# Two layers of image-prompt cross-attention: even entries with their image tokens first, three value groups instead of four where two token tiles can share one, and five score products instead of six

## The chip, the core and the metric

The kernel runs on one core of a Trainium2 chip. The core has five instruction streams that the profile names: PE (TensorE, matrix products; its weight loads are listed apart as PEld), DVE (VectorE), ACT (ScalarE), POOL (GpSimd) and SP (SyncE, which here only issues DMAs). Data lies in SBUF (128 partitions), products land in PSUM banks, and DMAs move data between SBUF and DRAM. The metric is the time of one execution on the device in microseconds (us).

## What is computed

The reference runs two attention layers over a batch of B = 16 entries with S = 256 queries, 20 heads of 16 dimensions, and a context of 256 tokens per entry (512 features). The time goes to these lines; the first layer is

```python
text = encoder_hidden_states[:, :TEXT_LEN]     # TEXT_LEN = 77
ip = encoder_hidden_states[:, TEXT_LEN:]       # 179 image tokens
q = hidden_states @ Wq
k_text, v_text = text @ Wk, text @ Wv
logits = einsum('bhqd,bhkd->bhqk', q_h, k_h) * scale
text_out = softmax(logits) @ v_h
ip_k, ip_v = ip @ Wk_ip, ip @ Wv_ip
scores = einsum('bhqd,bhkd->bhqk', q_h, ip_k_h) * scale
text_probs = softmax(q @ k_text.T * scale)     # over all 320 columns, no heads
q_sem = text_probs @ text
sem = (q_sem @ ip.T) * scale
ip_probs = softmax(scores + SEM_SCALE * sem) * spatial_mask
out = (text_out + ip_probs @ ip_v_h) @ Wout + bout + hidden_states
```

The second layer takes this output, has 252 text and 4 image tokens, and uses a similar semantic term on normalized vectors. So in layer one an entry's 256 context tokens are 77 that go through the text weights (Wk, Wv) and 179 that go through the image weights (Wk_ip, Wv_ip).

## The kernel before, in words

**Numbers.** A product of two 32-bit arrays is made from rounded halves: each array is split into a high part `hi` and a rest `lo`, and `prod` sums hi·hi, hi·lo and lo·hi over the blocks of the contraction; with 4 blocks of 128 features that is 12 products for one result. ACT writes the high part (`nc.scalar.copy`), DVE or POOL subtracts it to get the rest (`halves`). The last 64 of the 320 projected columns are stored as 64 high and 64 low weight columns side by side, so that a third block of columns (`m == 2`) gives both halves of its result in the two halves of the partitions; `evacuate` adds them.

**Stages.** `begin` loads the first weights and context and computes the first two entries by hand order. Layer one then runs in 80 slots (16 entries times 5 groups of 4 heads, `slot0`), layer two in 80 more (`slot1`). The name slot is a clock for a list of tasks: each task is a generator with a table of slot numbers, and `fill` runs every step that has come due. PE's order is fixed by this program order (`PINNED`), while the order of ACT, DVE, POOL and SP is chosen at build time by a scheduler that simulates the program.

**A slot of layer one.** For group `k` it does, in this order on PE: the transposed score products T of the first 128 tokens (`turned0`, tokens on partitions, queries along the row), a few task steps, the value products P·V of the group before (`attend0`, 24 products in sets of 4 side by side), the score products S of group `k + 2` (`score0`, queries on partitions, only to take the row maxima), T of the other 128 tokens, again task steps, and the small transposition of the maxima (`maxima0`). For S, DVE takes two maxima per head, one over text and one over image tokens. Four small DMAs on ACT's queue write the maxima as two more rows of the query stack (`qs`), where indicator rows of the key stack (`ks`) pick the right one. For T, ACT takes the exponential into a tile P and POOL multiplies it with `rs`, the exponential of the semantic term, so that P·V can follow. `settle0` transposes the result on DVE, divides by the sums, and POOL adds the text half and the image half into `hsn`; for the fifth group POOL copies that block once more (`hsn[:, 2, :, 1]`), and `gather` transposes `hsn` on DVE for the output projection (`finish`, PE lines 610 and 613, DVE lines 284 and 285).

**Token tiles.** An entry's 256 tokens stand text first, image behind. The first tile of 128 tokens holds 77 text and 51 image tokens, the second 128 image tokens. The value rows of the mixed tile are made twice, once with the text weights and once with the image weights, and a mask per partition keeps the right rows (`tmask`): three groups of 12 products per entry (`values0_`), six per pair. Columns 16, 33, ... of a value tile hold the mask itself and give the sums.

**Per pair of entries** (`c`, two entries of 512 tokens): `context` loads the context features in four chunks of 128x512 and splits them into `cta` and `ctb` (ACT high, POOL rest), `keys0` makes the key projections (three column blocks, text with 156 columns, image with 360) into `kst`, copies the text keys into `kb` on POOL, and writes `kst` to DRAM (`keys_out`), from where `stacks0` loads it in head order into `ks`. `tokens0` makes the 77x179 matrix M of text by image features (12 products of 192 columns), whose transposes give `rs`. `semantic0` makes the text scores over all 320 columns: per half of the queries six products (three column blocks, high and low of q) of 156 columns.

## Time and profile before

| what | value |
|---|---|
| median of 3 runs | 1497.43 us (1495.08 to 1497.73) |
| the profiled execution's own time | 1499.52 us |
| its span | 1497.7 us |
| PE instructions | 12740 products |
| layer one's slots after the start-up | from about 100 us to about 690 us |
| layer two's slots | about 700 us to 1450 us |

Engine rows give busy time in us, its share of the span and the count of instructions. In rows of groups the columns are: line and engine, operation, output <- inputs, shape, count, busy us in total, mean ns of one, and behind the bar the engine's idle time just before these instructions with what ended it. The mean ns of a product is its whole passage, and products overlap; the pace is read from the chain of waits, whose rows are start in us, length in us, engine, output, line and count of a run. In tables of stretches each engine has its busy us and its count of instructions, then the clock granted to PE, the busy share of the DMA engines and GB/s.

### The profile page before, as it was taken

The numbers are of one execution on the slowest core, as the hardware profiler recorded it, in microseconds if no ns is written. First come the engines' busy times: TensorE is split into PE (matmuls) and PEld (weight loads), VectorE is DVE, ScalarE is ACT, GpSimd is POOL, SyncE is SP. The second block draws the span as 40 slices with busy tenths as digits, with TensorE's granted clock in tenths as the row PEclk, the third lists the DMA queues.
The fourth block names the chain that finished last, engine by engine and source line by source line (L and its number), as shares of the span: only waits on it lengthen the run. The fifth ranks groups of instructions, "written<-read, shape, count | busy, mean of one in ns | idle before, by whom it ended". The sixth has DMA issues, their size and how long they took to land.

```text
span 1497.7 us, 36123 instructions
## 1 busy us (share of the span) xinstructions
PE 1427.8 (95%) x12740; PEld 1155.6 (77%) x12740; DVE 1170.2 (78%) x2593; ACT 884.8 (59%) x1975; POOL 1215.2 (81%) x1304
## 2 busy tenths in 40 slices
PE   8789999999999899789999999999999999999997
PEld 8678888888888778577777777777777777777765
DVE  5467777777777787878887788778877887788785
ACT  5346565656565555556666666666666666666562
POOL 4259797979797977887698879887988798879786
PEclk9799999999999999999999999999999999999999
DMA  7767787778787776775434434443444344433411
GB/s 237 201 185 217 201 228 200 217 206 224 199 231 193 219 200 173 186 216 150 145 102 132 127 108 128 127 127 108 127 128 127 109 126 129 127 108 103 122 26 39
DMA packets 230986, 234.32 MB, mean 156 GB/s; under 512 B 39127, under 2 KB 200678, under 8 KB 230790
## 3 DMA queue, kind: packets, MB, share of 16 engines
q1 hardware_dynamic: 228598, 230.71, 55.4%
q8 instruction: 102, 1.67, 0.5%
q10 hardware_dynamic: 2208, 1.30, 0.4%
q14 instruction: 78, 0.64, 0.1%
HBM read 118.04 MB, written 77.04 MB: 130 GB/s over the span
## 4 chain that ended last, share of the span: by engine, by line
PE 73%; DVE 8%; DMA 6%; POOL 6%; issue 3%; ACT 3%; SPq 1%; ACTq 0%; DVEq 0%; POOLq 0%
PE X L942 15%; PE X L240 14%; PE P L804 6%; PE X L610 5%; PE P L954 5%; PE S L745 5%; PE P L964 4%; PE T L769 4%; PE T L894 3%; PE S L900 3%; PE X L613 2%; PE X L250 2%; PE X L579 2%; POOL P L775 2%; DVE mn L747 1%
## 5 line engine op out<-in xcount | busy, mean ns | idle before, releaser
L775 POOL TENSOR_TENSOR P<-P,rs 128x512 f32<-128x512 f32 x320 | 414.4, 1318 | 90.2 <-ACT P L772 89.3
L933 POOL TENSOR_TENSOR wt<-P,ctb 128x512 f32<-128x512 f32 x320 | 410.6, 1308 | 72.8 <-ACT ctb L932 72.8
L942 PE MATMUL X<-ctb,gm 128*128 128x512 f32 x1120 | 305.4, 402 | 5.8 <-DVE wt L943 5.7
L772 ACT ACTIVATE P<-T 128x512 f32<-128x512 f32 x320 | 175.4, 594 | 159.5 <-PE T L769 101.9
L943 DVE TENSOR_TENSOR wt<-X,wt 128x512 f32<-128x512 f32 x320 | 216.1, 680 | 42.7 <-PE X L942 36.4
L942 PEld LDWEIGHTS X<-ctb,gm 128*128 128x128 f32 x1120 | 195.3, 188 | 39.0 <-DVE wt L943 8.7
L914 ACT ACTIVATE P<-T 128x512 f32<-128x512 f32 x320 | 173.0, 593 | 76.2 <-PE T L894 73.3
L932 ACT ACTIVATE ctb<-P 128x512 fp32r<-128x512 f32 x320 | 186.7, 627 | 36.8 <-PE X L942 33.1
L902 DVE TENSOR_REDUCE mn<-S 128x4 fp32r<-128x1008 f32 x160 | 191.3, 1196 | 0.0
L747 DVE TENSOR_REDUCE mn<-S 128x4 fp32r<-128x716 f32 x160 | 142.2, 889 | 0.0
L804 PE MATMUL P<-P,vr 128*32 128x256 f32 x1920 | 127.4, 396 | 5.3 <-DVE tmp L821 2.0
L745 PE MATMUL S<-ks,qs 125*128 125x256 f32 x640 | 117.7, 307 | 4.9 <-DMA ks<-M 2.8
L745 PEld LDWEIGHTS S<-ks,qs 125*128 125x128 f32 x640 | 89.0, 195 | 40.1 <-issue 20.9
L1031 POOL TENSOR_TENSOR r<-u,rs 128x40 f32<-128x40 f32 (+2 forms) x17 | 108.7, 6394 | 3.9 <-DVE u L1028 3.9
L769 PE MATMUL T<-qs,ks 127*128 127x256 f32 x640 | 108.2, 292 | 0.4 <-DMA qs<-mt 0.4
L746 DVE TENSOR_REDUCE mn<-S 128x4 fp32r<-128x308 f32 x160 | 74.4, 465 | 31.2 <-PE S L745 30.8
L815 DVE STREAM_TRANSPOSE nt<-P 128x512 f32<-128x512 f32 x80 | 56.9, 711 | 51.8 <-PE P L804 51.3
L769 PEld LDWEIGHTS T<-qs,ks 127*128 127x128 f32 x640 | 92.1, 198 | 2.0 <-DMA qs<-mt 1.0
L804 PEld LDWEIGHTS P<-P,vr 128*32 128x32 f32 x1920 | 57.2, 112 | 47.0 <-issue 8.1
L954 PE MATMUL P<-P,v1t 128*32 128x256 f32 x1280 | 85.7, 385 | 0.0
L964 PE MATMUL P<-wt,zone 128*32 128x256 f32 x1280 | 85.1, 381 | 0.3 <-DVE wt L943 0.3
L610 PE MATMUL X<-ho,wF 128*128 128x256 f32 x512 | 74.3, 287 | 6.5 <-ACT mt L755 4.0
(297 smaller groups left out, 2974.5 us busy)
## 6 DMA issues: line engine op xcount, KB each, us to landing
qd<-q SPq DMA_DIRECT2D x96, 256.0 KB
qs<-tph SPq DMA_DIRECT2D x64, 320.0 KB
rawc<-in_cT_dram SPq DMA_DIRECT2D x60, 256.0 KB
qs<-qd SPq DMA_DIRECT2D x80, 192.0 KB
ks<-kd SPq DMA_DIRECT2D x80, 192.0 KB
ks<-kd SPq DMA_DIRECT2D x160, 96.0 KB
qs<-qd SPq DMA_DIRECT2D x160, 96.0 KB
kd<-kst SPq DMA_DIRECT2D x57, 256.0 KB
```

The source lines that it names most:

```text
L240: last = mm(out, lhs(a, k), rhs(b, k), start=i == 0, stop=i == len(terms) - 1)
L745: mm(sp[:, h], Q[: XROW + T0, h, t * 128 : (t + 1) * 128], K[: XROW + T0, h], start=True, stop=True)
L769: mm(st[p][:, j], K[:KS0, 2 * p + j, t * 128 : (t + 1) * 128], Q[:KS0, 2 * p + j], start=True, stop=True)
L772: exp = anchor(nc.scalar.activation(pt, st[p], AF.Exp, scale=SCALE))
L775: anchor(nc.gpsimd.tensor_mul(pt, pt, rs[:, t : t + 1].to_broadcast([128, 2, S])))
L804: mm(pv[32 * s : 32 * s + 32, o : o + S], v[:, vt, h : h + 32], P[k, s // 2][:, t, s % 2], start=vt < 2, stop=vt != 1,)
L902: anchor(nc.vector.tensor_reduce(maxes[k + 2][:, t], sp[:, :, :T1], axis=AX.X, op=ALU.max))
L914: anchor(nc.scalar.activation(P[k, u][:, t], st[u], AF.Exp, scale=SCALE))
L932: nc.scalar.activation(R[k, u][:, t], P[k, u][:, t], AF.Copy, scale=0.5)
L933: anchor(nc.gpsimd.tensor_sub(W[k, u][:, t], P[k, u][:, t], f(R[k, u][:, t])))
L942: mm(yp, gm[:, gb], R[k, u][:, kt], start=i == 0, stop=i == len(blocks[n]) - 1)
L943: nc.vector.tensor_mul(W[k, u][:, n], yp, W[k, u][:, n])
```

## The change

Even entries of layer one are laid out with their 179 image tokens first and the 77 text tokens behind; odd entries stay text first. The even entry's second tile then holds 51 image tokens (rows 0 to 50) and 77 text tokens (rows 51 to 127), the odd entry's first tile 77 text tokens and 51 image tokens (rows 77 to 127). One group of 12 products whose 128 tokens are 51 image tokens of the even entry, 26 columns of zeros and 51 image tokens of the odd entry serves both mixed tiles (`values_mixed`); its result is evacuated twice, with the even and with the odd mask. To make these 128 tokens lie side by side, the context tiles get a layout of their own (51 zeros, then per half: text, text, image, 26 zeros, image, one zero), so the split into halves is done in two pieces per chunk, and image keys are evacuated entry by entry. `ks` gets 77 more columns: an even entry's key stack starts 77 columns later, so that the image columns of both layouts lie on the same place and the constant rows stay. Six other edits come along: the semantic scores use five products, since the last block of q now holds its high and low parts in the two halves of the partitions (and `kb` its text keys twice, by 8 small POOL copies instead of 3); M's product has 180 columns instead of 192; M's zeros are written once at the start instead of once per entry; the mask columns of the value tiles are written per entry (`mark`) instead of once; and the fifth group's block is written doubled by one DVE instruction, in layer one as the sum itself, in layer two as the product, instead of by a POOL copy.

```diff
@@ values
-        for t, (w,), lo, sc in ((0, wv0, 0, tmask[:, 0:1]), (1, wvi0, 0, tmask[:, 1:2]), (2, wvi0, 128, 1.0)):
-            prod(vp, lambda s, k: ct(s, k)[:, i, lo : lo + 128], lambda s, k: w(s, k), 4)
...
+    def value_rows(ct, at, w, *to):
+        vp = bank()[:, :320]
+        prod(vp, lambda s, k: side(ct[k], s, at, 128), lambda s, k: w(s, k), 4)
+        for V, t, sc in to:
             nc.scalar.activation(
                 vcols(V, V0W)[:, t, :, 0:16], vp.rearrange("p (h d) -> p h d", d=D), AF.Copy, scale=sc
             )
+    def values0_(b):
+        ct, i = ct0[b // 2], b % 2
+        V = mark(b)
+        value_rows(ct, T0 if i else -MIX, wv0[0], (V, 0, masks(b)[0]))
+        yield
+        value_rows(ct, CI + (CG + MIX if i else 0), wvi0[0], (V, 2, 1.0))
+        yield
         return V
+    def values_mixed(c):
+        to = [(vr[(b + 2) % 3], 1, masks(b)[1]) for b in (2 * c, 2 * c + 1)]
+        value_rows(ct0[c], CI + 128, wvi0[0], *to)
+        yield
@@ halves of a projected block
+    def evacuate(hi, lo, out, m, pieces=None, beside=False):
+        cut = [lambda t, b=b: t[:, b] for b in pieces] if pieces else [lambda t: t]
+        if m == 2:
+            hi, lo = hi[:64], hi[64:] if beside else lo[:64]
+            both = buf("both", list(hi.shape), bufs=2)
+        for of in cut:
+            nc.scalar.copy(of(hi), of(out[:64] if m == 2 else out))
...
+        for of in cut:
+            nc.vector.tensor_sub(of(out if m == 2 else lo), of(out), f(of(hi)))
@@ split of the context
+                if isinstance(hi, list):
+                    for piece in zip(hi, lo, by_side(src)):
+                        halves(*piece, eng, "pieces")
@@ keys
-                    nc.gpsimd.tensor_copy(kt[:n, m, :, :, :T0], f(kst[:n, :, :, :T0]))
+                    for h in range(2):
+                        for p in range(0, 128, n):
+                            nc.gpsimd.tensor_copy(kt[p : p + n, m, h, :, :T0], f(texts(kst)[:n, h]))
@@ M
-        nc.gpsimd.memset(f(M[:, :, :T0]), 0.0)
-        lo = 64
-        prod(gp[:T0, : S - lo], lambda s, k: ct(s, k)[:, i, :T0], lambda s, k: ct(s, k)[:, i, lo:S], 4)
+        prod(gp[:T0, : S - T0 + 1], lambda s, k: texts_of(ct[k], s)[:, i], lambda s, k: images_of(ct[k], s, 1)[:, i], 4)
@@ semantic scores
-            for k in range(3):
-                qt = lambda h: qh[:, h, k, t * 128 : (t + 1) * 128]
-                for h in range(2):
-                    mm(sf[:, : 2 * NT].rearrange("p (s n) -> p s n", s=2), qt(h), kt[:, k], start=k + h == 0, stop=k + h == 3)
+            for k, h in ((0, 0), (0, 1), (1, 0), (1, 1), (2, 0)):
+                qt = qh[:, h, k, t * 128 : (t + 1) * 128]
+                mm(sf[:, : 2 * NT].rearrange("p (s n) -> p s n", s=2), qt, kt[:, k], start=k + h == 0, stop=k == 2)
@@ stacks and scores
-        Q, K = QK[k] = qs[k % SIZES["NR"]], ks[k % SIZES["NR"]]
+        Q, K = QK[k] = qs[k % SIZES["NR"]], (ks if b % 2 else turned_ks)[k % SIZES["NR"]]
...
+        text, image = (slice(0, T0), slice(T0, S)) if k // NG % 2 else (slice(S - T0, S), slice(0, S - T0))
@@ P·V
-        for vt in range(3):
-            values0(k, pv, v, vt)
+        get("vm", b // 2)
+        for step in ((0, 0, 0, 1, 1), (1, 0, S, 1, 0), (2, 1, S, 0, 1)) if b % 2 else ((2, 0, S, 1, 0), (1, 1, S, 0, 1), (0, 1, 0, 1, 1)):
+            values0(k, pv, v, *step)
@@ settle0
-        nc.gpsimd.tensor_add(hn[:, g // 2, :, g % 2], tmp[:, 0], tmp[:, 1])
         if g == NG - 1:
-            nc.gpsimd.tensor_copy(hn[:, 2, :, 1], hn[:, 2, :, 0])
+            nc.vector.tensor_add(hn[:, 2], *[tmp[:, i].unsqueeze(2).to_broadcast([128, 8, 2, 16]) for i in range(2)])
             later(0.45, lambda: gather(0, b))
+        else:
+            nc.gpsimd.tensor_add(hn[:, g // 2, :, g % 2], tmp[:, 0], tmp[:, 1])
@@ settle1
         if g == NG - 1:
-            nc.gpsimd.tensor_copy(hn[:, 2, :, 1], hn[:, 2, :, 0])
+            wide = lambda t: t.unsqueeze(2).to_broadcast([128, 8, 2, 16])
+            nc.vector.tensor_mul(hn[:, 2], wide(na[:, :, 0:16]), rz.unsqueeze(2).unsqueeze(3).to_broadcast([128, 8, 2, 16]))
@@ the table of slots
-        task(("v0", 2 * c), shifted(n, -7, -5.4, -5), lambda b=2 * c: values0_(b), *k)
-        task(("v0", 2 * c + 1), shifted(n, -4, -3.8, -3.4), lambda b=2 * c + 1: values0_(b), *k)
+        task(("v0", 2 * c), shifted(n, -7, -5.4), lambda b=2 * c: values0_(b), *k)
+        task(("vm", c), shifted(n, -4.2), lambda c=c: values_mixed(c), *k)
+        task(("v0", 2 * c + 1), shifted(n, -3.8, -3.4), lambda b=2 * c + 1: values0_(b), ("vm", c))
```

The order of the instructions moves at three places that the prediction speaks of. Rows give the line, the operation, output <- inputs and the shape; `x3` is a run of three alike.

First PE, where the even entry of a pair got its two image value groups between a T and the transposition of the maxima (`wD` holds the image value weights, `cta` and `ctb` the context, `X` is a PSUM bank, `S` and `T` are the score products). Before:

```order
L769 MATMUL T_67<-qs2_97,ks2_101 128x256 x2
L240 MATMUL X_2214<-wD_93,cta_0_81 128x320 x3
L240 MATMUL X_2214<-wD_93,cta_1_82 128x320 x3
L240 MATMUL X_2214<-wD_94,ctb_0_83 128x320 x3
L240 MATMUL X_2214<-wD_94,ctb_1_84 128x320 x3
L240 MATMUL X_2230<-wD_93,cta_0_81 128x320 x3
L240 MATMUL X_2230<-wD_93,cta_1_82 128x320 x3
L240 MATMUL X_2230<-wD_94,ctb_0_83 128x320 x3
L240 MATMUL X_2230<-wD_94,ctb_1_84 128x320 x3
L753 MATMUL X_2248<-ident_r_79,mn_0_566 8x128 x2
L745 MATMUL S_66<-ks1_100,qs1_96 128x256 x4
```

and now:

```order
L861 MATMUL T_67<-qs2_97,ks2_101 128x256 x2
L251 MATMUL X_2265<-wD_93,cta_0_81 128x320 x3
L251 MATMUL X_2265<-wD_93,cta_1_82 128x320 x3
L251 MATMUL X_2265<-wD_94,ctb_0_83 128x320 x3
L251 MATMUL X_2265<-wD_94,ctb_1_84 128x320 x3
L845 MATMUL X_2285<-ident_r_79,mn_0_613 8x128 x2
L836 MATMUL S_66<-ks1_100,qs1_96 128x256 x4
```

One of two groups of 12 is gone there; the rest of PE's order in the slot is the same.

Second DVE, after the last group of an odd entry, around the transposition `hT` of the collected result `hsn` (`mn` are the maxima of S, `nt` and `tmp` belong to `settle0`, `ho` is the split of `hT` for the output projection). Before:

```order
L747 TENSOR_REDUCE mn_0_566<-S_66 128x4
L818 RECIPROCAL P_69<-nt_0_135 128x16
L834 STREAM_TRANSPOSE hT_0_1300<-hsn_109 128x256
L819 TENSOR_TENSOR P_69<-P_69,mk_106 128x8
L821 TENSOR_TENSOR tmp_1_808<-nt_0_135,P_69 128x256
L284 TENSOR_TENSOR ho_0_161<-hT_0_1300,ho_0_161 128x512
```

and now:

```order
L913 TENSOR_TENSOR tmp_0_847<-nt_1_137,P_69 128x256
L327 SCALAR_TENSOR_TENSOR hq_0_268<-hq_0_268,tmask_80,xq_0_91 128x256
L780 TENSOR_TENSOR tph_0_303<-X_1326,tph_0_303 77x256
L915 TENSOR_TENSOR hsn_110<-tmp_0_847 128x256
L838 TENSOR_REDUCE mn_0_613<-S_66 128x4
L839 TENSOR_REDUCE mn_0_613<-S_66 128x4
L927 STREAM_TRANSPOSE hT_0_1333<-hsn_110 128x256
L326 TENSOR_TENSOR ho_0_193<-hT_0_1333,ho_0_193 128x512
```

The sum for the fifth group is now DVE's own instruction (`hsn<-tmp`), and the last `hT` and `ho` come half a slot earlier in DVE's order.

Third SP, the queue of loads for the next groups (`x1d` takes layer one's output of an entry, `ks` and `qs` are the stacks). Before:

```order
L85 DMA ks_100<-kd_70 48x4x256
L85 DMA qs_96<-qd_1418 48x1024
L85 DMA x1d<-xc_116 128x3x256
L85 DMA ks_101<-M_261 80x4x179
L85 DMA ks_101<-kd_70 48x4x256
L85 DMA xq_91<-in_xT_dram 128x3x256
L85 DMA qs_97<-tph_264 80x4x256
L85 DMA qs_97<-qd_1418 48x1024
```

and now:

```order
L89 DMA qs_96<-qd_1456 48x1024
L89 DMA ks_101<-M_173 80x4x179
L89 DMA ks_101<-kd_70 48x4x256
L89 DMA xq_91<-in_xT_dram 128x3x256
L89 DMA qs_97<-tph_304 80x4x256
L89 DMA qs_97<-qd_1456 48x1024
L89 DMA x1d<-xc_117 128x3x256
L89 DMA ks_102<-kd_70 48x4x256
```

The output of an even entry is now issued behind five loads of the next group's stacks instead of ahead of them.

188 lines of the change are left out of this document (120 added, 68 removed).

## The prediction

> **What bounds the kernel now.** I read the page's busy times first, then busy time by stage, then single slots of one pair in layer one, and last the chain of waits there.
>
> ```profile
> span 1497.7 us, 36123 instructions
> ...
> PE 1427.8 (95%) x12740; PEld 1155.6 (77%) x12740; DVE 1170.2 (78%) x2593; ACT 884.8 (59%) x1975; POOL 1215.2 (81%) x1304
> ```
>
> PE is busy 95% of the span and POOL, next, 81%. The second view says where PE is not busy:
>
> ```profile
> 0.00:100.00 100.00, 79.35 (x531) 70.82 (x531) 54.88 (x142) 47.08 (x118) 43.50 (x66) 0.91 0.77 219
> 100.00:550.00 450.00, 438.93 (x4138) 378.19 (x4136) 346.62 (x811) 262.96 (x619) 391.56 (x380) 0.99 0.76 210
> 550.00:700.00 150.00, 131.34 (x1205) 105.03 (x1204) 116.66 (x259) 82.72 (x192) 124.33 (x145) 0.94 0.68 184
> 700.00:1450.00 750.00, 741.22 (x6606) 575.53 (x6606) 623.09 (x1319) 475.98 (x1016) 620.85 (x674) 1.00 0.42 118
> ```
>
> From 100 to 550 us layer one runs evenly: PE works 438.93 of 450 us. Start-up (79.35 of 100) and the passage to layer two (131.34 of 150) have the gaps. So a product that leaves PE between 100 and 550 us shortens the kernel, if the other engines keep up in the shorter slot. The third view is ten slots of one pair; three of them, and the sum of the ten:
>
> ```profile
> 307.70:315.10 7.40, 6.58 (x65) 5.78 (x63) 7.32 (x15) 4.66 (x10) 5.84 (x6) 1.00 0.76 201
> ...
> 330.00:337.40 7.40, 7.40 (x73) 6.47 (x72) 3.90 (x10) 3.58 (x9) 5.14 (x6) 1.00 1.01 266
> ...
> 344.90:352.40 7.50, 7.45 (x73) 6.46 (x72) 6.10 (x13) 5.61 (x12) 7.46 (x9) 1.00 0.72 199
> ...
> sum 74.50, PE 72.81 PEld 63.18 DVE 57.42 ACT 43.54 POOL 64.91; mean PE 7.28 PEld 6.32 DVE 5.74 ACT 4.35 POOL 6.49
> ```
>
> A pair lasts 74.5 us. PE's share is 72.81, POOL's 64.91, DVE's 57.42. But single slots differ: DVE is full from 307.7 (7.32 of 7.40, and PE loses 0.82 there), POOL from 344.9 (7.46 of 7.50). Now the chain around the place where the order of PE loses a group (value products are `L240 x12` or `x24`, the semantic scores `L667`):
>
> ```profile
> 241.17 2.86 PE X L240 x24
> 244.16 0.53 PE S L745 x4
> ...
> 248.68 1.30 PE X L667 x12
> 250.10 0.52 PE S L745 x4
> ...
> 254.27 3.52 PE X L240 x24
> 257.91 0.53 PE S L745 x4
> ```
>
> The chain goes through PE from slot to slot, and both kinds of removed products lie on it. One slot, S to S, takes 257.91 − 250.10 = 7.81 us with the two value groups in it, and 250.10 − 244.16 = 5.94 with the semantic scores.
>
> **The change part by part.** *Value groups.* 24 products of 320 columns take 3.52 us, 147 ns each. A pair loses one group of 12: 12 × 0.147 = **1.76 us**.
>
> *Semantic scores.* 12 products of 156 columns take 1.30 us, 108 ns each. A pair loses one of six per half of the queries, in two halves and two entries: 4 × 0.108 = **0.43**. The 128-row block that replaces a 64-row one costs the same columns.
>
> *M.* 24 products per pair get 180 columns instead of 192. At 3.52/24/320 = 0.46 ns a column that is 24 × 12 × 0.46 ns = 0.13; where the pace is set by the weights, as 108 ns for 156 columns (0.69 a column) suggests, it is nothing. Between 0 and 0.13 I take 0.12, as 192 columns lie on the long side of those 156. Text keys of 154 columns instead of 156: nothing.
>
> Sum on PE: 1.76 + 0.43 + 0.12 = **2.3 us a pair**, 18.5 over eight pairs, if all of it reaches the end.
>
> *POOL.* These are the prices; T's products with `rs` (`L775`), the sum into `hsn` (`L822`), its copy (`L824`), and the small work:
>
> ```profile
> L775 POOL TENSOR_TENSOR P<-P,rs 128x512 f32<-128x512 f32 x319 | 413.1, 1318 | 81.9 <-ACT P L772 80.9
> L822 POOL TENSOR_TENSOR hsn<-tmp 128x128 f32<-128x128 f32 x80 | 41.0, 513 | 5.6 <-DVE tmp L821 5.1 <-DVE mx L674 0.5
> L168 POOL TENSOR_TENSOR cta<-rawc,cta 128x512 fp32r<-128x512 f32 x16 | 21.6, 1354 | 0.0
> L385 POOL CAST kb<-kst 128x308 fp32r<-128x308 f32 x14 | 6.2, 441 | 0.8 <-DVE rn L460 0.8
> L824 POOL COPY hsn<-hsn 128x128 f32<-128x128 f32 x16 | 4.8, 300 | 0.1
> L435 POOL MEMSET M<- 77x154 f32 x12 | 2.7, 227 | 5.0 <-PE X L697 4.8
> ```
>
> A split chunk of 512 columns becomes two pieces of 154 and 358: the columns are the same, so each of four chunks costs one more start of an instruction, at most the 0.227 of the smallest row: +0.9. Three casts of `kb` (441) become eight of half the size, each between 0.227 and 0.3 (the copy of 128 columns): +0.5 to +1.1. Four copies of mask columns (128x20): 4 × 0.227 = +0.9. Gone are two copies (0.60), two sums (1.03) and two memsets of M (0.45): −2.08. POOL gets **+0.2 to +0.8 a pair**, against 74.5 − 64.91 = 9.6 idle. Per slot POOL needs four products and a sum, 4 × 1.318 + 0.513 = 5.79. The slot that loses 1.76 shrinks to 7.81 − 1.76 = 6.05, still 0.26 above, and one of 5.94 passes already. POOL's idle time in this slot is 7.40 − 5.14 = 2.26, of this shape:
>
> ```profile
> 335.28 2.52 POOL L775 TENSOR_TENSOR P<-P,rs 128x512 f32<-128x512 f32 x2 [2.12 <-ACT P L772]
> ```
>
> POOL waits 2.12 there for ACT, thus for PE; it eats that wait first. What it gives back lies between nothing and 1.76 (the slot stays as long as it is); as most of the wait remains coverable and the neighbour at 344.9 is full, I take **0.5 a pair**.
>
> *ACT.* Split and image keys come in more pieces. ACT is the idlest (43.54 of 74.50 us busy), so a start of some 0.2 each, five or so a pair, is hidden; with the cover gone, 1 us a pair, inside what is given back in the second rival.
>
> *DVE.* Two sums of the fifth group per pair move over, doubled to 256 elements, and three pieces of keys are added. The nearest rows:
>
> ```profile
> L821 DVE TENSOR_TENSOR tmp<-nt,P 128x256 f32<-128x256 f32 x80 | 33.2, 415 | 1.4
> L834 DVE STREAM_TRANSPOSE hT<-hsn 128x256 f32<-128x256 f32 x51 | 21.8, 428 | 14.7 <-POOL hsn L822 11.7 <-POOL hsn L824 1.6 <-POOL hsn L1014 1.4
> L168 DVE TENSOR_TENSOR kst<-X,kst 128x358 fp32r<-128x358 f32 x14 | 7.4, 530 | 8.5 <-ACT kst L165 8.4
> L284 DVE TENSOR_TENSOR ho<-hT,ho 128x512 fp32r<-128x512 f32 x16 | 17.7, 1105 | 8.5 <-ACT ho L283 8.5
> ```
>
> `L821` has the size of the new sum, 0.42; a wait goes in return: DVE stood 11.7 us before the transposition for POOL's sum and 1.6 for its copy, 13.3/16 = 0.83 per entry. What is behind DVE in that wait, the maxima `mn` and the next `settle0`, comes earlier. Three key pieces add 3 × 0.15 (a third of 530) at worst. Net: 2 × (0.42 − 0.83) + 0.45, about −0.4 on DVE, which PE covers; I book **nothing** in the even stretch.
>
> *SP.* `x1d` moves behind five loads for the next groups, which come earlier by its issue:
>
> ```profile
> 278.00 0.60 SPq L85
> ```
>
> `x1d` is a store to DRAM that only layer two reads, so late by five such issues (3 us) it delays nobody in layer one; at the passage it could, once, for the last even entry. Earlier loads could win 0.6 twice a pair where the chain passes SP. Both are left at **nothing**.
>
> *Start-up.* The chain there is loads:
>
> ```profile
> 3.55 5.34 DMA raw<-in_cT_dram
> ...
> 39.85 5.80 DMA qs<-qd
> 45.67 6.25 DMA rawc<-in_cT_dram
> ```
>
> The removed products of pair 0 are hidden under such waits: 0. The pieces and memsets of the start cost between 0 and 2 (some eight small ones at 0.227 of the memset row); POOL works 43.50 of 100 us there, so I take **+0.3**.
>
> *Pair 7 and the passage* (550 to 700 us): PE is busy 131 of 150, 88%, and half of the time the chain goes elsewhere. I take half of 2.3: **−1.2**; and **+0.5** for DVE's two sums, which lie bare where the chain runs through the output of the last entry (bounds 0 and 2 × 0.42).
>
> *Layer two.* The product of the fifth group doubles on DVE (0.2 more, half of `L821`), 16 times, and a copy of 0.300 leaves POOL. PE is busy 741.22 of 750: hidden, **0**; bare it would be 16 × 0.2 = 3.2.
>
> Six pairs lie between 100 and 550 us (450/74.5): 6 × (2.3 − 0.5) = **−10.9**. Sum: −10.9 − 1.2 + 0.3 + 0.5 = −11.3. The profiled execution took 1499.5 us (its span 1497.7 and 1.8 around it), so 1488.2; the median of the runs is 2.1 lower, 1497.4, so **1486**.
>
> **The rivals.** *Two-input sums block POOL (slower).* The same DVE subtraction of 128x512 exists alone and beside a busy POOL:
>
> ```profile
> L1267 DVE TENSOR_TENSOR cta<-rawc,cta 128x512 fp32r<-128x512 f32 x2 | 1.4, 692 | 3.9 <-ACT cta L1260 3.9
> ```
>
> ```profile
> 273.24 1.66 DVE L284 TENSOR_TENSOR ho<-hT,ho 128x512 fp32r<-128x512 f32 x1 [1.36 <-ACT ho L283]
> ...
> 274.31 0.92 POOL L822 TENSOR_TENSOR hsn<-tmp 128x128 f32<-128x128 f32 x1
> ```
>
> At the start it takes 692 ns, later 1105 in the mean and 1.66 us here, while POOL's sum of 0.513 took 0.92. The new sums have two such operands. If each cost 1.66 instead of 0.42 and POOL lost 0.92 − 0.51 = 0.41 behind it, all bare, that is 1.65 × 16 = 26.4 us against −11.3: about **1513**. It decides once a sum eats DVE's slack of a slot, 7.45 − 5.74 = 1.7 in the mean but 0.08 in the slot at 307.7. Against it: `L821`, two inputs as well, 80 times, holds 415 in the mean, and the sum behind it can't run before. Chance 0.12.
>
> On this the Trainium skill speaks against the change: "SBUF — State Buffer", section "Who interferes with whom", says that a VectorE instruction with two SBUF inputs contends with a GpSimd one that reads SBUF, and whoever is later waits. By that rule each new sum could wait for one product `L775`, 1.318 us; the trace agrees for `L284`, less for `L821`. Sixteen bare waits of that length would be 21 us and the time about 1507, inside the rival above.
>
> *POOL sets the slot.* The chain ACT → POOL → P·V is what a slot waits for as soon as PE is short: then the shortened slot stays at 7.81 and the value groups bring nothing in the six pairs. A like wait is the way of the maxima to `qs`:
>
> ```profile
> 404.20 3.54 PE X L240 x24
> ...
> 408.09 0.35 ACT mt L755
> 408.47 0.57 ACTq L757
> ...
> 409.95 5.29 DMA qs<-mt
> ...
> 415.29 0.82 PE T L769 x3
> ```
>
> From the maxima to T it takes 7.2 us behind those 24 products, and T waits. With 12 products the transposition comes 1.76 earlier, and so does T, unless the DMAs (1.01 of their time busy from 330.0) get no faster. Left is 6 × (0.43 + 0.12) = 3.3, less 1 for pieces: −2.3, about **1495**. Against it: slots of 5.94 run now. Chance 0.15.
>
> *Everything is kept.* −18.5 in eight pairs: **1479**. For it, the waits before POOL; against it, start-up and passage. Chance 0.08.
>
> *Odd starts.* Even key stacks begin 77 words later. Should operands at odd words double the pace of 0.53/4 = 0.13 us, the 320 S and 320 T products of even entries bring 640 × 0.13 = +83 on 1486: about **1569**. No row speaks for it; against it, the value columns begin at steps of 17 words, odd ones too, and their loads show nothing odd:
>
> ```profile
> L804 PEld LDWEIGHTS P<-P,vr 128*32 128x32 f32 x1920 | 57.2, 112 | 47.0 <-issue 8.1
> ```
>
> Chance 0.03.
>
> **How the numbers follow.** Forecast 0.62, rivals 0.12, 0.15, 0.08 and 0.03. The forecast's own span is 1481 (give-back nil) to 1491 (give-back 1.5). To hold 8 in 10 the range takes in "everything kept" and the 1495 of POOL: 1478 to 1498. About 0.2%, 3 us, can be told from no change: faster are the forecast, everything kept and a little of the POOL rival, 0.73; the same is most of that rival, 0.12; slower 0.15.
>
> **What would show it.** PE's count falls by 128 to 12612 at the same pace (3.52 for 24 and 0.108 for 156 columns), and the pair shrinks from 74.5 to about 72.7. The slot of 7.81 becomes 6.05 to 6.5. POOL's wait of 2.12 there becomes some 0.4 to 0.9. Before `hT` DVE's wait of 11.7 for POOL is nearly gone, and the new sum stands at 0.42 (at 1.0 or more the first rival is at work, and `L822` above 0.6). Four products of S keep 0.53. Layer two keeps its 750 us. The forecast is wrong if the pair stays above 74, or if PE's idle time between 100 and 550 us grows by more than 5 us.

## The result, and the profile after

The changed kernel takes **1518.55 us** (median of 6 runs, 1506.46 to 1522.68) against 1498.07 of the kernel before on the same chip (6 runs): a ratio of **1.012**, interval 1.008 to 1.0161. The forecast was 1486, range 1478 to 1498. It is slower by 20 us where 11 were to be gained.

The page of the profiled run, span and busy times:

```profile
span 1521.0 us, 36145 instructions
...
PE 1428.7 (94%) x12612; PEld 1148.5 (76%) x12612; DVE 1226.0 (81%) x2641; ACT 888.3 (58%) x2031; POOL 1210.5 (80%) x1358
```

PE has the 128 products less that were foreseen (12612). But DVE is busy 1226.0 us instead of 1170.2: 56 us more for 48 instructions. By stage (span, then busy us and count of PE, PEld, DVE, ACT, POOL, granted clock, DMA share, GB/s):

```profile
0.00:100.00 100.00, 75.83 (x495) 69.59 (x495) 53.13 (x146) 46.51 (x128) 43.15 (x97) 0.85 0.76 210
100.00:550.00 450.00, 426.83 (x3974) 363.28 (x3972) 372.06 (x829) 261.04 (x652) 383.15 (x411) 0.98 0.76 206
550.00:700.00 150.00, 131.57 (x1163) 105.00 (x1164) 121.06 (x262) 79.88 (x187) 120.66 (x137) 0.92 0.73 184
700.00:1450.00 750.00, 732.53 (x6462) 566.96 (x6461) 626.51 (x1294) 467.69 (x1004) 606.20 (x658) 1.00 0.44 121
```

From 100 to 550 us PE now stands idle 23 us instead of 11, and in layer two, which was to stay as it was, 17 instead of 9 of 750. The time is lost in three places, the start, layer one and layer two, read from the starts of the first P·V product of each slot:

| | before | after |
|---|---|---|
| first P·V of layer one | 66.9 us | 70.1 us |
| pair 0 of layer one | 89.4 us | 93.6 us |
| pairs 1 to 4 of layer one, each | 74.5, 75.4, 74.5, 75.0 us | 77.4, 78.2, 76.2, 73.0 us |
| first P·V of layer two | 696.6 us | 708.7 us |
| a pair of entries in layer two, middle | 99.9 us | 102.3 us |
| first to last P·V of layer two | 772.1 us | 786.8 us |

Pairs are counted from 0. The two spans lie 23.3 us apart: 3.2 of it is the start, 4.2 pair 0, 5.4 pairs 1 to 4 and 14.7 layer two; pairs 5 to 7 and the end are 4.2 shorter together. One pair of layer one, pair 4, takes the forecast 73 us. The groups of DVE that grew, first of the kernel before and then of the changed one, from 100 to 700 us (count, busy us, mean ns, and behind the bar the wait ahead of them):

```profile
L285 DVE SCALAR_TENSOR_TENSOR hq<-hq,tmask,xq 128x256 fp32r<-128x256 f32 x15 | 8.8, 589 | 2.0 <-ACT hq L283 1.9
L284 DVE TENSOR_TENSOR ho<-hT,ho 128x512 fp32r<-128x512 f32 x15 | 17.0, 1133 | 8.5 <-ACT ho L283 8.5
```

```profile
L327 DVE SCALAR_TENSOR_TENSOR hq<-hq,tmask,xq 128x256 fp32r<-128x256 f32 x15 | 20.6, 1372 | 2.0 <-ACT hq L325 1.9
L326 DVE TENSOR_TENSOR ho<-hT,ho 128x512 fp32r<-128x512 f32 x15 | 20.4, 1357 | 6.7 <-ACT ho L325 6.7
L927 DVE STREAM_TRANSPOSE hT<-hsn 128x256 f32<-128x256 f32 x45 | 19.3, 428 | 0.0
L915 DVE TENSOR_TENSOR hsn<-tmp 128x256 f32<-128x256 f32 x15 | 16.1, 1073 | 0.2
```

The new sum `hsn<-tmp` takes 1.07 us here (1.16 over all 16), not 0.42; the wait before `hT` is gone, as foreseen. Of the instructions that both kernels have, the one that grew most is one that the change doesn't touch: DVE's part of the split of the queries, `hq`, which POOL does for the first two blocks (L326) and DVE for the last (L327). Its mean hides two values. Here are two entries of layer one in the changed kernel, DVE and POOL apart. The first, in pair 2 (78.2 us):

```profile
295.50 3.45 DVE L327 SCALAR_TENSOR_TENSOR hq<-hq,tmask,xq 128x256 fp32r<-128x256 f32 x1 [0.38 <-ACT hq L325]
298.87 0.41 DVE L913 TENSOR_TENSOR tmp<-nt,P 128x256 f32<-128x256 f32 x1
```

```profile
293.41 3.78 POOL L867 TENSOR_TENSOR P<-P,rs 128x512 f32<-128x512 f32 x3
297.13 1.28 POOL L326 TENSOR_TENSOR hq<-xq,hq 128x512 fp32r<-128x512 f32 x1
298.33 0.33 POOL L464 CAST kb<-kst 128x154 fp32r<-128x154 f32 x1
299.36 0.46 POOL L918 TENSOR_TENSOR hsn<-tmp 128x128 f32<-128x128 f32 x1 [0.69 <-DVE tmp L913]
```

and in pair 4 (73.0 us):

```profile
450.35 0.48 DVE L327 SCALAR_TENSOR_TENSOR hq<-hq,tmask,xq 128x256 fp32r<-128x256 f32 x1 [0.39 <-ACT hq L325]
450.75 0.41 DVE L913 TENSOR_TENSOR tmp<-nt,P 128x256 f32<-128x256 f32 x1
```

```profile
447.95 4.04 POOL L867 TENSOR_TENSOR P<-P,rs 128x512 f32<-128x512 f32 x3
451.96 1.28 POOL L326 TENSOR_TENSOR hq<-xq,hq 128x512 fp32r<-128x512 f32 x1
```

At 295.50 DVE comes upon a POOL that has work queued without a gap; it stands until POOL's third product, its `hq` and a copy into `kb` are done, 3.45 us, and POOL pauses only where it has to wait for DVE's `tmp` itself. At 450.35 it runs at once in 0.48, and POOL's product pays (three take 4.04 instead of 3.78). Behind it on DVE wait `tmp` and the maxima. In layer two the same instruction meets POOL's part of the same split:

```profile
962.75 0.60 DVE L285 SCALAR_TENSOR_TENSOR hq<-hq,tmask,xq 128x256 fp32r<-128x256 f32 x1
```

```profile
963.01 1.50 POOL L284 TENSOR_TENSOR hq<-xq,hq 128x512 fp32r<-128x512 f32 x1
```

before, DVE 0.26 us ahead; and after, POOL 0.01 ahead:

```profile
980.49 1.56 DVE L327 SCALAR_TENSOR_TENSOR hq<-hq,tmask,xq 128x256 fp32r<-128x256 f32 x1
```

```profile
980.48 1.29 POOL L326 TENSOR_TENSOR hq<-xq,hq 128x512 fp32r<-128x512 f32 x1
```

Here whoever comes first runs at full or nearly full speed, and the other waits. In layer one it is less simple: three POOL instructions that start after 295.50 run ahead of the DVE instruction that came before them. I call such a meeting a tie, won or lost by DVE.

### The profile page after: what moved, and what is told of

The parts are those of the page before. It is cut to its first block, busy times and chain, and to the rows that moved or that the text cites. A ratio compares the mean times of both kernels' runs of the same rounds, so it can differ in the third digit from the quotient of the medians.

```text
span 1521.0 us, 36145 instructions
## 1 busy us (share of the span) xinstructions
PE 1428.7 (94%) x12612; PEld 1148.5 (76%) x12612; DVE 1226.0 (81%) x2641; ACT 888.3 (58%) x2031; POOL 1210.5 (80%) x1358
## 4 chain that ended last, share of the span: by engine, by line
PE 59%; DVE 16%; POOL 9%; DMA 7%; issue 5%; ACT 2%; SPq 2%; ACTq 0%; DVEq 0%; POOLq 0%
PE X L251 12%; PE X L1035 11%; PE P L896 6%; PE X L701 5%; PE S L836 4%; PE P L1047 3%; POOL wt L1026 3%; PE P L1057 3%; PE T L861 3%; DVE wt L1036 3%; PE S L993 3%; POOL r L1124 3%; DMA qs<-qd 2%; PE T L987 2%; DVE mn L839 2%
## 5 line engine op out<-in xcount | busy, mean ns | idle before, releaser
L1007 ACT ACTIVATE P<-T 128x512 f32<-128x512 f32 x320 | 173.5, 595 | 75.9 <-PE T L987 73.6
L838 DVE TENSOR_REDUCE mn<-S 128x4 fp32r<-128x308 f32 x160 | 74.5, 466 | 35.0 <-PE S L836 34.8
L1057 PE MATMUL P<-wt,zone 128*32 128x256 f32 x1280 | 84.4, 379 | 0.0
L271 ACT CAST kst<-X 128x179 fp32r<-128x179 f32 (+5 forms) x117 | 36.0, 329 | 80.7 <-PE X L251 46.1
L993 PE MATMUL S<-ks,qs 48*128 48x256 f32 x640 | 75.4, 313 | 8.0 <-DVE mn L995 7.7
```

What stands on the lines that cost most here:

```text
L1007: anchor(nc.scalar.activation(P[k, u][:, t], st[u], AF.Exp, scale=SCALE))
```

## The experiments

All ratios are to the kernel before on the same chip in the same set of runs. The sets are copy2 to doubling, here2 to here2psum, hqpool to here2mx, and start to onekb; from one set to another the ratios are to be compared.

| run | median us | ratio and interval |
|---|---|---|
| copy2 | 1522.84 | 1.0140 (1.0095 to 1.0186) |
| idle2 | 1523.37 | 1.0143 (1.0094 to 1.0192) |
| copies | 1543.67 | 1.0275 (1.0219 to 1.0332) |
| doubling | 1496.56 | 0.9960 (0.9928 to 0.9992) |
| here2 | 1507.51 | 1.0053 (1.0028 to 1.0078) |
| beside2 | 1511.93 | 1.0073 (1.0051 to 1.0095) |
| six | 1516.13 | 1.0095 (1.0055 to 1.0134) |
| here2psum | 1510.91 | 1.0064 (1.0037 to 1.0092) |
| hqpool | 1500.12 | 0.9998 (0.9979 to 1.0017) |
| hqpoolpsum | 1498.52 | 0.9988 (0.9965 to 1.0011) |
| hqpoolmx | 1510.90 | 1.0086 (1.0063 to 1.0108) |
| here2mx | 1525.81 | 1.0174 (1.0156 to 1.0192) |
| start | 1518.57 | 1.0129 (1.0096 to 1.0162) |
| one | 1491.75 | 0.9948 (0.9926 to 0.9969) |
| onenp | 1497.06 | 0.9979 (0.9954 to 1.0003) |
| onekb | 1507.30 | 1.0042 (1.0011 to 1.0073) |

How much a comparison shows depends on the order of the instructions, which the build plans anew for ACT, DVE, POOL and SP. The traces have it unchanged in here2 and beside2 (against the changed kernel and the kernel before), and but for the edited instructions themselves in idle2 and start (against the changed kernel), one (against hqpoolpsum) and onenp (against hqpool). In copy2 it is unchanged in layer one. In the other runs it differs from that of the kernel they start from, so there an edit comes with another order.

### Is it the fifth group's block, doubled by DVE?

My first theory was that POOL, freed of a copy, comes earlier and wins the tie. `copy2` takes the edit of layer two back:

```diff
-            nc.vector.tensor_mul(hn[:, 2], wide(na[:, :, 0:16]), rz.unsqueeze(2).unsqueeze(3).to_broadcast([128, 8, 2, 16]))
+        nc.vector.tensor_mul(hn[:, g // 2, :, g % 2], na[:, :, 0:16], rz.unsqueeze(2).to_broadcast([128, 8, 16]))
+            nc.gpsimd.tensor_copy(hn[:, 2, :, 1], hn[:, 2, :, 0])
```

> The changed kernel with one of its edits undone: in layer two the fifth group's block is again a product of 128 elements on DVE and a copy on POOL. Theory A (POOL, freed of a copy of 0.29 us, reaches its part of the split of the queries 0.03 us ahead of DVE's part instead of 0.25 behind it, and DVE then takes 1.57 instead of 0.57 us, once in each entry of layer two): DVE's part of that split is back near 0.57, a pair of entries of layer two takes 99.9 instead of 102.3 us, and the whole is 14 to 17 us shorter than the changed kernel, about 1503. Theory B (layer two is slower for another reason: the buffers, or what layer one left behind): pairs stay at 102 us, the whole within 4 us of 1518. Layer one stays as it is under both.

`idle2` keeps DVE's product and gives POOL the copy back, to no use:

```diff
+            nc.gpsimd.tensor_copy(buf("idle", [128, 8, 16], bufs=1), hn[:, 2, :, 0])
```

> The changed kernel with DVE's doubled product of layer two kept, and POOL's copy of 128x128 put back beside it, into a tile that nobody reads. The order on DVE, ACT and SP is that of the changed kernel. Theory A (what counts is when POOL reaches its part of the split of the queries): pairs of layer two near 100 us, the whole 12 to 17 us shorter than the changed kernel, although there is more work. Theory C (the longer product on DVE, 0.42 instead of 0.29 us, is what layer two pays for): pairs stay at 102 us or more, the whole at 1518 or above.

`copies` takes the doubling back in both layers:

> The changed kernel with the doubling on DVE undone in both layers: sum and copy of the fifth group on POOL again, so that the value groups, the semantic scores, the layout and the small edits remain. Theory A (DVE's sums with two SBUF operands at 1.16 instead of 0.42 us, and the ties they bring with POOL, ate the gain of layer one): layer one's pairs near 73 us instead of 77, layer two's 99.9, the whole near 1486, as forecast. Theory D (in layer one the pieces and small copies on POOL, or the later start of the even key stacks, cost more than PE saves): layer one's pairs stay at 75 to 78 and the whole stays above 1498.

and `doubling` is the kernel before with the doubling of both layers alone:

> The kernel before with one part of the change alone: the fifth group doubled by DVE in both layers, no copy on POOL. Theory A (the doubling alone makes the loss): slower than the kernel before by 15 to 30 us, pairs of layer two near 102.3, DVE's sum near 1.16 us in layer one. Theory D (the loss of layer one comes from the other edits): layer one's pairs at 74.5 to 75, only layer two slower, by up to 17 us.

Theory A fell in all four. Pairs of layer two stay at 102.3 us in copy2 and idle2, and `hq` of layer two at 1.45 and 1.49 us. Theory C's numbers are met in idle2, but copy2, without the longer product, has the same. In copies they stay too, and layer one gets worse (78 to 86 us a pair, `hq` up to 3.88, PE idle 37 of 450 us); DVE's and POOL's orders differ there from the change, and what makes it worse than the change wasn't settled. It isn't `hq` alone: pairs 1 and 3 of copies take 78.4 and 79.5 us with 0.65 and 1.11 for it. And doubling alone makes the kernel faster, not slower: layer two at 99.9, layer one's pairs 74.6, 74.6, 74.7, 74.6, although its sum takes 0.88 us in the mean, 0.42 and 1.18 by turns. So the sum's contention, real as it is, doesn't make the loss by itself. Why the doubling gains was not tried.

### Where DVE writes the rest of q

What remains for layer two is an edit that belongs to the five semantic products: the rest of q's last block is written to the upper half of the partitions, in layer two as well, where nobody needs it. Two rows before and two after the add, first in the kernel before:

```profile
946.54 0.67 DVE L943 TENSOR_TENSOR wt<-X,wt 128x512 f32<-128x512 f32 x1
947.14 0.41 DVE L262 TENSOR_TENSOR q<-X,both 64x256 fp32r<-64x256 f32 x1
947.47 0.16 DVE L869 COPY sq<-S 128x16 f32<-128x16 f32 x1
947.55 1.19 DVE L902 TENSOR_REDUCE mn<-S 128x4 fp32r<-128x1008 f32 x1
```

and after:

```profile
964.01 0.67 DVE L1036 TENSOR_TENSOR wt<-X,wt 128x512 f32<-128x512 f32 x1
964.72 0.42 DVE L278 TENSOR_TENSOR q<-X,both 64x256 fp32r<-64x256 f32 x1
965.17 0.17 DVE L962 COPY sq<-S 128x16 f32<-128x16 f32 x1
965.26 1.20 DVE L995 TENSOR_REDUCE mn<-S 128x4 fp32r<-128x1008 f32 x1
```

From `wt` to `q` it is 0.60 before and 0.71 after, from `q` to `sq` 0.33 and 0.45. The add no longer overlaps its neighbours on either side, and the maxima are 0.24 us later for it. `here2` puts the rest back into its half in layer two alone:

```diff
-            evacuate(qh[:, 0, m], qh[:, 1, m], pp, m, beside=True)
+            evacuate(qh[:, 0, m], qh[:, 1, m], pp, m, beside=l == 0)
```

(with the store that reads it). 

> The changed kernel with one thing undone in layer two only: DVE's add that makes the rest of the last block of q (L278) writes to the lower half of the partitions again, where its inputs are, and no longer to the upper half. The order of the instructions is the same on all engines. Theory E (an add whose output lies in the other half of the partitions starts 0.12 us later and holds up the next by as much; the maxima and with them PE are 0.27 us late, DVE then comes to its part of the split of the queries 0.03 us behind POOL instead of 0.27 ahead, and loses 1.0 us more): that part is 0.57 us again, pairs of layer two take 99.9 instead of 102.3 us, the whole is 14 to 18 us below the changed kernel; layer one stays at 73 to 78 a pair. Theory F (the place of q's rest means nothing; layer two is slow by a chance in the order or by addresses): pairs stay at 102.3.

`beside2` does the reverse, to the kernel before:

> The kernel before with that one thing added in layer two only: the rest of q's last block is written to the upper half of the partitions. The order of the instructions is the same on all engines, and no work is added. Theory E: DVE's part of the split of the queries in layer two goes from 0.57 to about 1.57 us, a pair from 99.9 to 102.3, the whole 14 to 18 us slower than the kernel before. Theory F: no difference, within 3 us.

In both the order of every engine's instructions is that of the kernel they start from. Layer two's `hq` in here2 and then in beside2:

```profile
L327 DVE SCALAR_TENSOR_TENSOR hq<-hq,tmask,xq 128x256 fp32r<-128x256 f32 x14 | 8.7, 619 | 0.0
```

```profile
L285 DVE SCALAR_TENSOR_TENSOR hq<-hq,tmask,xq 128x256 fp32r<-128x256 f32 x13 | 19.8, 1523 | 0.0
```

here2's pairs take 99.9 us, beside2's 102.3. Theory E holds both ways; first to last P·V of layer two is 775.2 and 785.6 us. The changed kernel itself has a case: in pair 4 of its layer two DVE wins in one of the two entries (0.48 us at 1185 us), and that pair takes 101.3 instead of 102.3. The whole moves by 11 us in each (medians, here2 to the changed kernel in another set of runs), less than the 14 I had said.

> The changed kernel with the edit of the semantic scores undone in both layers: six products per half again, the rest of q's last block in the lower half, six small copies into kb instead of eight. Theory E for layer one as well (the same late add loses the tie of DVE's part of the split of the queries, 3.3 instead of 0.48 us in every second entry): that part is 0.5 us everywhere in layer one, pairs at 73 us, layer two at 99.9; the whole near 1486, below the kernel before by 8 to 14 us. Theory G (in layer one DVE's sum with two SBUF operands at 1.16 us, or the order found by the planner, is what costs): layer one's pairs stay at 75 us or more, and only layer two's 16 us come back, about 1502.

In `six`, with six products and no rest in the upper half in either layer, layer two comes back (99.9), layer one does not: `hq` 3.3 to 3.5 in every second entry, pairs of 78.1 to 78.7. So in layer one the tie is lost for another reason than the place of q's rest. The whole, 1516.13, is neither E's 1486 nor G's 1502: layer two starts at 714.8 us, 6 later than in the change.

### The two operands of the new sum

`here2psum` makes the fifth group's product in two halves, one to SBUF and one to PSUM:

```diff
+            ab = [tmp[:, 0], pv[:, 16:144].rearrange("p (f d) -> p f d", d=16)]
+            for i in range(2):
+                nc.vector.tensor_mul(ab[i], nt[:, i, :, 0:16], rz[:, i].unsqueeze(2).to_broadcast([128, 8, 16]))
+            nc.vector.tensor_add(hn[:, 2], *[t.unsqueeze(2).to_broadcast([128, 8, 2, 16]) for t in ab])
```

> As the first of these (rest of q's last block in its own half in layer two), and the sum of the fifth group made from one operand in SBUF and one in PSUM, for which its product is done in two halves. Theory H (two SBUF operands are what makes the sum take 1.16 us beside POOL; the rows of 0.42 had an operand in PSUM): the sum is 0.42 us in every entry, the two half products 0.28 each, and DVE's busy time falls by about 9 us; the time falls by 2 to 8 us against the first of these. Theory I (the sum is slow for its doubled output, or waits): it stays above 0.8.

The sum takes 0.40 to 0.42 us in all 16 entries instead of 0.4 to 2.4: theory H holds for the instruction. The time doesn't follow: 1510.91 against 1507.51, where 2 to 8 us less were expected. Set side by side, the profiled runs of the change, here2 and here2psum tell about layer one, though (length of the pair, and the second of DVE's two `hq` in it):

| pair | the change | here2 | here2psum |
|---|---|---|---|
| 1 | 77.4, 3.25 us | 75.7, 3.29 us | 73.0, 0.48 us |
| 2 | 78.2, 3.45 | 73.7, 0.48 | 76.8, 3.36 |
| 3 | 76.2, 3.28 | 77.4, 3.37 | 78.2, 3.32 |
| 4 | 73.0, 0.48 | 77.3, 3.32 | 78.5, 3.44 |

Each pair in which DVE wins is 73.0 to 73.7 us long, each in which it loses 75.7 to 78.5.

The traces hold a cleaner comparison. The changed kernel, here2, copy2, idle2 and start run pairs 1 to 4 with the same instructions in the same order. Of these 20 pairs DVE wins this tie in two, at 73.0 and 73.7 us, and loses it in 18, at 75.7 to 78.3. The 18 fall into two groups by the clock granted to PE: at 1.00 five pairs take 75.7 to 76.3 us, at 0.96 to 0.98 thirteen take 77.1 to 78.3. So a lost tie comes to 2 to 3 us at the full clock, and to one or two more where the granted clock fell as well; whether the clock falls because PE waits isn't shown.

### The tie of layer one taken away

`hqpool` starts from here2 and lets POOL do the last block of the queries too, in layer one:

```diff
-        order(nc.vector.scalar_tensor_tensor(hl[:, 2], f(hl[:, 2]), neg, src[:, 2], op0=ALU.mult, op1=ALU.add))
+            order(eng.tensor_sub(hl[64:, 2], src[64:, 2], f(hl[64:, 2])))
```

> The run with q's rest in its own half in layer two (here2), and in layer one DVE's part of the split of the queries (L327 on hq, two operands in SBUF) done by POOL instead, as a subtraction on the 64 partitions that need it. Theory J (in layer one DVE's part loses the tie with POOL in most pairs, 3.3 instead of 0.48 us, and that is what layer one lost): pairs 1 to 5 all take 73 to 74 us instead of 75.7, 73.7, 77.4, 77.3, 76.8, the whole falls by 10 to 16 us against here2, to 1491 to 1497. Theory K (POOL is the bound of layer one, or the other two-operand work of DVE beside POOL is enough to hold it): pairs stay at 75 to 78, and POOL's added 0.7 us per entry makes them longer, the whole at 1507 or more.

`hqpoolpsum` adds the sum from SBUF and PSUM:

> The same, and the sum of the fifth group from one operand in SBUF and one in PSUM (0.41 instead of 1.2 us, with its product in two halves of 0.28). Theory J: what DVE saves beside POOL, about 0.6 us an entry, is partly on the path: 0 to 8 us below the run before it. Theory K: no change within 3 us, since POOL sets the pace.

hqpool falls to the time of the kernel before (ratio 0.9998), 7.4 us below here2 in another set: theory J in direction, short of its 10 to 16. Pairs are 74.5, 73.2, 74.9, 76.3; in the three longer ones now the sum of the fifth group loses (2.40 to 2.51 us). hqpoolpsum has 73.4, 73.3, 73.2, 72.6, what the forecast had, and still only 1498.52; that is 1.6 us below hqpool, which J and K both allow. Its first P·V comes at 70.5 us instead of 66.9, and its last two pairs take 88.0 and 79.6 instead of 85.8 and 75.6. Its stretch from 100 to 550 us:

```profile
100.00:550.00 450.00, 434.25 (x4133) 371.42 (x4126) 368.27 (x858) 267.70 (x671) 407.31 (x440) 1.00 0.79 213
```

PE idles 16 us there, against 11 before and 23 in the change. Are the removed products worth what I said? `hqpoolmx` does the mixed group's 12 products twice:

```diff
-        prod(vp, lambda s, k: side(ct[k], s, at, 128), lambda s, k: w(s, k), 4)
+        for again in to:
+            prod(vp, lambda s, k: side(ct[k], s, at, 128), lambda s, k: w(s, k), 4)
```

> The first of these, with the 12 products of the mixed group done twice (the second result replaces the first, so nothing else changes): PE does four image value groups per pair again. Theory J (once the ties are out of the way PE sets the pace, and a removed group is worth its 1.76 us): pairs 1 to 5 take 74.7 to 75.5, the whole is 8 to 14 us above the first of these. Theory K (PE has room): no change within 3 us.

It takes 1510.90, 10.8 us above hqpool. My term was 6 × 1.76 = 10.6 and half of one 1.76 for pair 7. For the whole theory J holds. Pair by pair it doesn't: pairs 1 to 4 take 75.9, 75.9, 74.5 and 78.2 us, which is 1.4, 2.7, −0.4 and 1.9 more than in hqpool, and the order of the other engines differs. So the 10.8 speaks for the term, but doesn't measure it by itself.

> The run here2 (DVE's part of the split of the queries on DVE as in the change), with the 12 products of the mixed group done twice. Theory L (the shorter PE work moved DVE against POOL, and that is why the tie is lost in layer one): with PE's work back the part takes 0.5 to 0.8 us again in most entries and the pairs 74.5 to 75.5, so the whole is the same as here2 or a little less, 1500 to 1507. Theory M (the pieces and small copies on POOL moved POOL, not PE): the part stays at 3.3 us, pairs at 77 to 79, the whole at 1510 to 1520.

`here2mx` missed both. With PE's work back, DVE wins in pairs 2 to 4 (0.48 each; 74.7, 75.0, 75.8 us), but loses in two earlier entries by 6.20 and 6.09, more than ever, and these pairs take 97.7 and 81.8. Which way a tie falls depends on small shifts of either engine.

What sets the length of a long loss can be read from the traces. In all 36 entries in which this `hq` took over 2 us, it ended 0.28 us behind the last of a row of POOL instructions that follow each other without a pause: at 295.50 the row ends with the copy into `kb`, in here2mx it goes on through two more products. Which way a tie falls shows in part. In layer one after 100 us DVE's `hq` came 187 times while POOL worked on a product with `rs`. With at most 0.24 us of that product left it was done in 0.46 to 0.50 us, 109 times of 111. With more left it got through at the end of that product 42 times (0.28 us behind it) and had to wait for POOL's pause 34 times. What decides between these two isn't told by these runs.

### The start

With both ties repaired (hqpoolpsum) four pairs were 1.1 to 2.4 us shorter, the start 3.6 us longer, and the whole was equal. The issue queue of SP in the start-up, kernel before and then the change (start, length of the run of issues, and the count at the end of the row):

```profile
17.24 3.17 SPq L85 DMA_DIRECT2D ks<-mt  x4
20.47 0.75 SPq L85 DMA_DIRECT2D M<-mt  x1
```

```profile
17.40 6.79 SPq L89 DMA_DIRECT2D ks<-mt  x8
24.24 0.70 SPq L89 DMA_DIRECT2D M<-mt  x1
```

The shifted key stack needs its constant rows 77 columns further, and the change writes these by four DMAs of their own. They take SP 3.6 us, and every load and store that SP issues from there on stands behind them. `start` is the change with one DMA for both parts:

```diff
-            dma(ks[i][XROW + T0 : KS0, :, :T0], ind0r[:2, :T0].unsqueeze(1).to_broadcast([2, 4, T0]))
-            dma(ksw[i][XROW + T0 : KS0, 4 * S :], ind0r[:2, :T0])
+            five = bass.AP(four.tensor, four.offset, [list(four.ap[0]), [S, 5], [1, T0]])
+            dma(five, f(ind0r[:2, :T0]).unsqueeze(1).to_broadcast([2, 5, T0]))
```

> The changed kernel, with the constant rows of the key stacks written by four DMAs of SP (2x5x77) instead of eight (2x4x77 and 2x77); nothing else is moved. Theory N (SP issues the eight in 6.79 us where four took 3.17, and all of the start stands behind them): the first product of P.V starts 3 to 3.6 us earlier, near 67 us instead of 70.1, and the whole is about 3 us shorter than the changed kernel, save what the ties with POOL add or take away. Theory O (the start is later because of POOL's and ACT's small pieces): the first P.V stays at 69 to 70.

The first P·V comes at 68.0 us instead of 70.1, so 2.1 of the 3.2 come back, between what N and O expected; the four DMAs take SP 3.95 us here. The whole is 1518.57: nothing is seen of it there. This profiled run loses the tie in pair 4 as well (3.40, 77.6 us).

> All four repairs together: q's rest in its own half in layer two, the last block of the queries' split on POOL in layer one, the sum of the fifth group from SBUF and PSUM (these are hqpoolpsum), and the constant rows by four DMAs. Theory N: about 3 us below hqpoolpsum, 1494 to 1497, so 3 to 6 us below the kernel before, with pairs 1 to 4 at 73.3. Theory O: as hqpoolpsum, 1498.

> The same with DVE's sum of the fifth group left as in the change (both operands in SBUF). If the sum costs only when it meets POOL: 0 to 4 us above the run before this one.

`one` takes **1491.75 us, ratio 0.9948 (0.9926 to 0.9969)**: below both kernels. Pairs 1 to 4 are 72.8, 73.7, 73.4, 72.6, the first P·V of layer two comes at 689.5 us (696.6 before), and from 100 to 550 us PE does more in the same time than in the change (4105 products for 3974):

```profile
100.00:550.00 450.00, 432.46 (x4105) 370.27 (x4106) 367.52 (x860) 267.39 (x672) 405.53 (x441) 1.00 0.79 214
```

one differs from hqpoolpsum in SP's DMAs alone. Its first P·V comes 2.5 us earlier; its last two pairs are 3.6 and 2.7 us shorter as well, for which no cause was looked for. The 0.5% that one gains on the kernel before also has to be set beside doubling: that one edit alone has 0.9960 (0.9928 to 0.9992), so the runs don't tell the whole change with four repairs from it.

`onenp`, with the sum left on two SBUF operands, lies 5.3 us above (expected 0 to 4), its intervals overlapping with one's. Against hqpool, from which it differs in SP's DMAs alone, it goes from 0.9998 to 0.9979.

> All four repairs, and the text keys copied to kb by four copies of POOL per pair (two halves of the rest in one) instead of eight: 4 x 0.2 us less on POOL per pair. Where POOL is next to bound layer one, up to 0.8 us a pair, 5 us in all, below the run with four repairs; otherwise no change within 3 us.

`onekb` has less work on POOL and is 15.6 us slower than one. Layer one's middle pairs take 73.9 to 75.0, pair 5 takes 83.5 and pair 6 88.3 (79.0 and 84.4 in one). DVE's parts of `ho` take longer in places (up to 2.85 us for an instruction of 0.47), but the orders of several engines differ from one's, and the cause was not tried further. It stays open.

## Why the prediction was wrong, point by point

- **Value groups and what PE saves.** Right. A pair without a lost tie takes 73.0 us (72.7 foreseen). In that pair the slot of 7.81 us takes 6.18 (6.05 to 6.5 foreseen), and POOL's wait in it is 0.40 (0.4 to 0.9). Putting the products back costs 10.8 us (10.6 foreseen for six pairs), though unevenly by pair. PE's count was right, and its pace too: the 12 products that are left take 1.76 us.
- **"Semantic scores ... A pair loses 4 × 0.108 = 0.43", and nothing against it.** This is the step that failed first. The edit pays for its product by placing q's rest in the other half of the partitions; I read the five products and not the add that feeds them, and did not see that it applies to layer two, where I had booked "hidden, 0" for the doubled product alone. The add and the late maxima cost 0.24 us by the rows, and the lost tie 1.0 more: 2.4 us a pair, 10 to 15 us in layer two. here2 and beside2 show it both ways. This is the largest single part of the miss.
- **"L821 has the size of the new sum, 0.42."** The size is right, the operands are not. Half of `L821`'s input, `P`, lies in PSUM; the sum reads SBUF twice. The nearest row was `L284` with 1105 ns, and the sum took 1.16 (18.6 us in 16). The bounds of 0.42 and 1.66 hold for the mean; single sums took up to 2.47. My reason against the rival, "two inputs as well, 80 times, holds 415", was the same mistake. Taking the contention away in here2psum moved the time by nothing that can be told, and the doubling alone gains; but where `hq` is out of the way, a lost sum lengthens a pair (hqpool).
- **The rival "two-input sums block POOL".** It gave the right side, 1513 for 1518.55, by a near mechanism at another place: mainly not the new sums and not POOL waiting, but DVE waiting in `hq`, which was there before. That the numbers lie so close is luck, since the rival had nothing for layer two. It has no threshold in DVE's slack as I had it; it depends on a few tenths of a microsecond between the two engines. On this the Trainium skill ("SBUF — State Buffer", section "Who interferes with whom") says that the order of issue, not the shape of the operation, decides who blocks; the rows at 962.75 and 980.49 agree (0.60 and 1.56 us for the same instruction). The row at 295.50 doesn't: there POOL instructions that start after DVE's run ahead of it, 3.45 us in all, and the measurement decides. I had read that section and priced the added instruction by it, not the instructions that it would shift.
- **The 0.5 a pair given back, in 6 × (2.3 − 0.5).** Mis-sized: three of the four middle pairs gave back all and 1.7 to 2.9 us more, by the tie of `hq` (3.3 instead of 0.48); pair 0 lost 4.2. That POOL's order of work has a say was right; what POOL does to DVE I had counted only for the sum. Why the change loses this tie is open: PE's shorter work alone doesn't do it (here2mx still loses, then wins), nor q's rest (six), nor the sum (here2psum).
- **"Start-up +0.3".** Mis-sized: +3.2 us, of it about 2.1 by four DMA issues on SP that are in the change and that I did not count; I had priced memsets there. The rest is not told apart; the clock granted to PE up to the first P·V was lower too, 0.83 against 0.91.
- **Rivals "POOL sets the slot", "odd starts", "everything is kept".** None of them. The slot of 7.81 did shrink to 6.18, so POOL doesn't set it. In `one`, with the same odd starts, the pairs take 73 us, so odd starts cost nothing visible; products of S keep their mean (307 and 312 ns).
- **What would show it.** "At 1.0 or more the first rival is at work" was met by the sum (1.07), but not its second half, POOL's sum above 0.6: it takes 0.459 in the mean. "PE's idle time grows by more than 5 us" was met by 12.
- **Small slips.** The row at 241.17, 24 products in 2.86 us, isn't two value groups but 12 products of M and 12 of the text values; no term hangs on it. The sixth score product that leaves was no 64-row one: all 192 of the kernel before stand in its trace with 128 rows, 274 ns in the mean. By its own terms the forecast's span for a give-back of nothing to 1.5 is 1483 to 1492, not 1481 to 1491.

## What to carry to other kernels

Where two engines hold each other up, as DVE and POOL do here, look up for each two-operand instruction where its operands lie, and treat each meeting of two such instructions as a tie that a shift of a tenth or two of a microsecond may turn: list those that are already in the kernel, not only the new ones. An edit that moves the place of data (another half of the partitions, another column) is to be followed through the instruction that writes it, all callers of the helper, and the DMAs that fill its constant parts. When a change with a sound gain comes out slower, take its side edits away one by one, and keep the order of the instructions where you can: here the runs that kept it gave the clear answers. Putting the main edit's products back cost 10.8 us, and still the change came out ahead, by 0.5%, only with four small repairs.

## What the runs showed of the hardware

- DVE's add from partitions 0 to 63 to partitions 64 to 127 starts 0.11 us later and holds the next instruction 0.12 us longer than the same add within its half (0.71 and 0.45 us against 0.60 and 0.33).
- A DVE instruction with two operands in SBUF that loses to POOL can wait for several POOL instructions, also for some that start after it: 3.25 to 3.45 us in the changed kernel, 6.20 in here2mx, for 0.48 of work. In 36 of 36 such long waits it ended 0.28 us behind the end of POOL's row without a pause. With one operand in PSUM the sum was 0.40 to 0.42 in all 16 entries.
- The DMAs of two rows here cost the issuing queue 0.8 to 1.0 us each (3.17 us for four, 6.79 for eight, 3.95 for the four of start).
- Pairs of layer one in which PE was granted the full clock and DVE lost the tie took 75.7 to 76.3 us; where the granted clock was 0.96 to 0.98, 77.1 to 78.3.
- One and the same kernel scatters: 1506 to 1523 us for the changed kernel, 1488 to 1495 for `one`, but also 1495 to 1514 for the kernel before in the last set. That lost ties make the scatter is not shown: each kernel has one profile.
